# Two GNN layers on one Trainium2 core: re-ordered queues at the start, in layer 0's loop and in the last stages

## The chip, the cores and the metric

The kernel runs on one core of one Trainium2 chip. The metric is the device time of one execution in microseconds; the time before is the median of three runs. Five engines work side by side, each with an instruction queue that the program fills in order: PE multiplies matrices, DVE and POOL work on vectors, ACT applies functions, and SP issues DMAs. ACT can issue DMAs as well.

## The reference, cut to what matters

All numbers are 32-bit floats. x holds 64 batches of 256 nodes with 512 features; the adjacency is 256 x 256; attention has 8 heads of 64.

```python
# layer 0
h = relu(layernorm(x))
x = x + einsum('nm,bmd->bnd', adj, h) @ W0 + b0
# layer 1
h = relu(layernorm(x))
q, k, v = h @ Wq + bq, h @ Wk + bk, h @ Wv + bv          # 8 heads of 64
scores = q k^T / 8 + (1 - adj) * -1e9
x = x + (softmax(scores) @ v) @ Wo + bo
```

## The kernel before, in words

**Groups.** The 64 batches are worked on in 32 groups of two. Layer 0 is done for all groups first and leaves its residual and its hidden values in DRAM; layer 1 then reads them group by group.

**Products with fewer multiplications.** Almost every large product is done in a seven-product scheme of the Strassen-Winograd kind. Its operands are sums of quarters: of the weights s1 to s4, of the features t1 = b12 - b11, t2 = b22 - t1, t3 = b22 - b12 and t4 = b21 - t2. From group 2 on, layer 1 applies the scheme a second time inside some of the seven products, which are named A to G; for the output projection ("o") C, D, E and F are split again, A, B and G are not. The sums for that second level are the block sums: those of the weights are made once (`block_sums`, line 327 or 597 in the profile), those of the features per group (`Blocks.sums`, line 597).

**Clock and delays.** The program is written out by hand in steps. `tick()` ends a step; `after(n, fn)` puts an operation into the queues n ticks later, in the order of due time and then of entry. So a delay is no waiting time: it decides which instructions stand ahead of the operation in its engine's queue. `behind_seeds` and `behind_scores` are lists of work put into the queues at fixed places of `score`.

**Start.** `load(0)` issues eight DMAs of 128 KB on SP, four for each of the two batches; ACT issues the adjacency in four and then the bias. `turn_adjacency` copies and transposes the adjacency (lines 377 to 384). `first_ready` normalizes the first group tile by tile: `moments` on DVE (lines 42, 43), `power` on DVE and POOL (62, 63), `shift` on DVE (69, called nb), the ReLU on ACT (842). `first_adjacency` (line 897) then multiplies with the adjacency.

**Layer 0's loop.** In the step loop of group g, PE alternates between w_g, the weight product of group g (line 505, banks w_ga, w_gb, w_gc), and py of group g+1, its adjacency product (line 950). Meanwhile `ready(g+2, ...)` prepares the group after next: moments on DVE, the scales on POOL (lines 51 to 54), four ReLUs on ACT (871), then `feature_sums` and `last_feature_sum` on POOL (934, 937; called hs). POOL also makes t1 to t4 of y (line 498; t3 overwrites a quarter of yT and shows as yT<-yT) and, as each batch is finished, the scales of h1 (51 to 54 again, two columns wide). ACT applies h1's ReLUs (1000), DVE transposes h1 (1006, `turn`), and SP stores residual (1010) and hidden (1015) and loads a later group's x (346).

**Layer 1's loop.** For every group: two attentions (`attend`: the denominators pden at 1218, the product with v at 1225), each followed by scores (`score`, 1166) and by a stage of projections. The order within such a stage is a string of tokens: `QK`, `VO`, `V1`, and for the last stages `O1` (outputs of group 30) and `OL` (outputs of group 31). A token such as oFc is one instruction of product F of "o"; "|" is a tick; "x" is the next exponent if one is due. `score` reads its banks on DVE (1174, 1177), subtracts the upper bound "top" (1182 on DVE, 1184 or 1186 on POOL), takes exponents on ACT (1202) and sums over keys on POOL (1209). After an attention, 1/den is made (`invert`, 1240 to 1244; for the very last one partly by DVE's reciprocal, 1248), then `divide` (1263) writes OT, from which the t's of the outputs are made (`HO[g].sums`, line 498) and the block sums (`block_outputs`).

In the last group, scores come first, then four of O1's eight sections, then the last attention, then the rest of O1, and OL.

## Time and profile before

| what | us |
|---|---|
| median of 3 runs (2617.2 to 2618.22) | 2618.0 |
| the profiled execution, its own time | 2618.1 |
| its span, first to last instruction | 2616.3 |
| PE busy | 2587.3 |
| POOL busy | 2077.2 |
| DVE busy | 1910.3 |
| ACT busy | 1379.8 |

In a line of the timeline or of the groups one reads: start and duration (or busy time and mean), engine, line of the kernel, operation, written tile <- read tiles, shape, count, and in brackets how long the engine was idle before it and what ended that. A line of the waits reads: who waited, for whom, total, times, longest. A matrix product of 32-bit floats shows as two instructions. PE's ends are modelled, so its busy time can hold short waits.

### The profile page before, as it was taken

How to read it: one execution, taken by the hardware profiler on the slowest of the kernel's cores; microseconds unless marked ns; L12 is line 12 of the kernel's file. 1: busy time of each engine (PE TensorE's matmuls, PEld its weight loads, DVE VectorE, ACT ScalarE, POOL GpSimd, SP SyncE). 2: the span in 40 equal slices, each digit the busy share in tenths (PEclk: the TensorE clock that was granted, in tenths of full speed). 3: DMA queues.
4: the chain of work that ended last, by engine and by line, in shares of the span. 5: the costliest groups of instructions: out<-in, count | busy, mean ns of one | idle time of the engine just before them, and what ended most of it. 6: DMA issues, size and time to landing. Idle time of an engine off the chain costs nothing.

```text
span 2616.3 us, 57383 instructions
## 1 busy us (share of the span) xinstructions
PE 2587.3 (99%) x21876; PEld 2304.1 (88%) x21876; DVE 1910.3 (73%) x4165; ACT 1379.8 (53%) x3198; POOL 2077.2 (79%) x2259
## 2 busy tenths in 40 slices
PE   8999999999999999999999999999999999999998
PEld 7999899998888888888888888888888888888886
DVE  6888788875576677777776777777777777777776
ACT  4545454543455555555555555555555555555553
POOL 6788887774788888888877888888888888887785
PEclk9999999999999999999999999999999999999999
DMA  5776666664111222211111111111122221111101
GB/s 149 198 193 182 171 165 184 161 163 112 33 50 49 64 63 66 54 50 50 50 49 50 49 50 50 50 50 49 49 62 64 65 56 50 50 49 50 50 34 50
DMA packets 281111, 211.40 MB, mean 81 GB/s; under 512 B 145920, under 2 KB 212992, under 8 KB 280832
## 3 DMA queue, kind: packets, MB, share of 16 engines
q1 hardware_dynamic: 280224, 207.02, 29.9%
q8 instruction: 175, 2.87, 0.4%
q14 instruction: 104, 0.85, 0.1%
q10 hardware_dynamic: 608, 0.66, 0.1%
HBM read 106.96 MB, written 100.66 MB: 79 GB/s over the span
## 4 chain that ended last, share of the span: by engine, by line
PE 88%; POOL 5%; DVE 4%; DMA 2%; issue 1%; SPq 1%; ACT 1%; DVEq 0%; ACTq 0%; POOLq 0%
PE sc L1166 9%; PE pav L1225 8%; PE o_pa L662 4%; PE pden L1218 2%; PE v_pa L648 2%; PE q_pa L648 2%; PE k_pa L648 2%; PE v_pa L662 2%; PE o_pc L662 2%; PE q_pa L662 2%; PE k_pa L662 2%; PE o_pa L648 2%; PE v_pc L648 1%; PE q_pc L648 1%; PE k_pc L648 1%; DVE st L42 1%
## 5 line engine op out<-in xcount | busy, mean ns | idle before, releaser
L1174 DVE SCALAR_TENSOR_TENSOR a<-sc,top 128x512 f32<-128x512 f32 x256 | 159.0, 684 | 262.1 <-PE sc L1166 262.1
L1209 POOL TENSOR_TENSOR as<-a 128x512 f32<-128x512 f32 x256 | 320.4, 1281 | 7.8 <-ACT a L1202 6.2
L1186 POOL TENSOR_TENSOR a<-a,top 128x1024 f32<-128x1024 f32 x124 | 291.1, 2370 | 36.7 <-DVE a L1177 36.7
L1242 POOL TENSOR_TENSOR as<-as 128x512 f32<-128x512 f32 x64 | 80.9, 1264 | 275.1 <-ACT as L1241 264.3
L1202 ACT ACTIVATE a<-a 128x1024 f32<-128x1024 f32 x256 | 271.9, 1063 | 23.5 <-POOL a L1186 11.9
L1166 PE MATMUL sc<-q,k 64*128 64x256 f32 x2048 | 239.5, 383 | 0.0
L1166 PEld LDWEIGHTS sc<-q,k 64*128 64x128 f32 x2048 | 196.7, 187 | 43.3 <-issue 25.4
L1225 PE MATMUL pav<-a,v 128*32 128x256 f32 x4096 | 233.6, 379 | 0.0
L1225 PEld LDWEIGHTS pav<-a,v 128*32 128x32 f32 x4096 | 133.6, 110 | 87.8
L1232 ACT ACTIVATE as<-pden 128x512 f32<-128x512 f32 x64 | 38.3, 598 | 283.3 <-PE pden L1218 283.3
L42 DVE BATCH_NORM_STATS2 st<-x 128x6 f32<-128x512 f32 x256 | 173.2, 677 | 10.8 <-DMA x<-in_x_dram 8.0
L1177 DVE SCALAR_TENSOR_TENSOR a<-sc,maskT 128x512 f32<-128x512 f32 x256 | 158.3, 681 | 0.0
L306 ACT ACTIVATE sc<-maskT 128x512 f32<-128x512 f32 x256 | 137.5, 590 | 0.0
L1000 ACT ACTIVATE h<-x,nb,rs 128x512 f32<-128x512 f32 x128 | 97.2, 808 | 65.7 <-POOL nb L54 63.9
L871 ACT ACTIVATE h<-x,nb,rs 128x512 f32<-128x512 f32 x124 | 90.8, 803 | 65.4 <-POOL nb L54 62.3
L934 POOL TENSOR_TENSOR hs<-h 128x512 f32<-128x512 f32 x31 | 39.4, 1270 | 72.9 <-ACT h L871 71.1
L821 DVE TENSOR_TENSOR x<-o_pa,x 128x512 f32<-128x512 f32 (+1 forms) x121 | 82.4, 682 | 9.0 <-PE o_pa L662 5.2
L1263 DVE TENSOR_TENSOR oT<-pav,as 128x512 f32<-128x512 f32 x128 | 82.1, 683 | 9.2 <-POOL as L1244 9.2
L1087 ACT ACTIVATE q<-q_pa,bq_c 128x256 f32<-128x256 f32 (+1 forms) x150 | 61.7, 456 | 50.1 <-PE q_pa L648 37.6
L597 POOL TENSOR_TENSOR spare<-h1T,spare 128x128 f32<-128x128 f32 x180 | 82.2, 456 | 7.0
L1244 POOL TENSOR_TENSOR as<-as 128x512 f32<-128x512 f32 x64 | 81.0, 1265 | 5.4
L498 POOL TENSOR_TENSOR t_y<-yT,t_y 128x512 f32<-128x512 f32 (+1 forms) x65 | 82.2, 1265 | 3.4 <-ACT yT L906 1.0
(1637 smaller groups left out, 8741.1 us busy)
## 6 DMA issues: line engine op xcount, KB each, us to landing
x<-in_x_dram SPq DMA_DIRECT2D x256, 128.0 KB, 3.0
residual<-x SPq DMA_DIRECT2D x256, 128.0 KB, 2.5
hidden<-r SPq DMA_DIRECT2D x128, 256.0 KB, 4.5
h1T<-hidden SPq DMA_DIRECT2D x64, 512.0 KB, 7.4
x<-residual SPq DMA_DIRECT2D x32, 1024.0 KB, 7.9
out_dram<-x SPq DMA_DIRECT2D x62, 512.0 KB, 4.1
w_sb<-in_L_gnn_weight_dram SPq DMA_DIRECT2D x1, 1024.0 KB, 8.3
wq_sb<-in_L_gnn_Wq_dram SPq DMA_DIRECT2D x1, 1024.0 KB, 7.3
```

What stands on the lines that cost most here:

```text
L42: nc.vector.bn_stats(st, src)
L306: nc.scalar.mul(t, seed, times)
L648: nc.tensor.matmul(o[:, 0, :], lhs, rhs, start=bool(fresh), stop=True, skip_group_check=True)
L662: nc.tensor.matmul(t[:, m, :], lhs, rhs, start=starts, stop=True, skip_group_check=True)
L1000: nc.scalar.activation(h1[:, k * NT + t, :], xt[:, k * NT + t, :], AF.Relu, bias=nb[:, t:t + 1], scale=rs[:, t:t + 1])
L1166: nc.tensor.matmul(ps[j][:, kt * N:(kt + 1) * N], k[j * HD:(j + 1) * HD, c, kt * P:(kt + 1) * P], q[j * HD:(j + 1) * HD, c, :], start=(kt ...
L1174: nc.vector.scalar_tensor_tensor(o, ps[j].rearrange("p (k n) -> p k n", k=NT), SCALE, top_b[:, 0:NT, :], op0=ALU.mult, op1=ALU.subtract)
L1177: nc.vector.scalar_tensor_tensor(o.rearrange("p k n -> p (k n)"), ps[j], SCALE, maskT_f, op0=ALU.mult, op1=ALU.add)
L1186: nc.gpsimd.tensor_tensor(a, a, top_b, op=ALU.subtract)
L1202: nc.scalar.activation(a, a, AF.Exp)
L1209: nc.gpsimd.tensor_tensor(AS[c, b], a4[:, :, 0, :], a4[:, :, 1, :], op=ALU.add)
L1225: nc.tensor.matmul(po[f][h * 32:(h + 1) * 32, b * N:(b + 1) * N], v[:, k, h * HD + f * 32:h * HD + f * 32 + 32], A[h // 2, b][:, (h % 2) * ...
```

## The change

- Start: the first tile of x and the adjacency are issued alternately on SP and ACT, in the order first tile, adjacency, second tile. PE multiplies the identity by itself 11 times before the adjacency's transposes and 8 times after.
- For group 1, `shift` is put into the queue with the first ReLU instead of with the scales. Group 2's moments, scales and last feature sum take later steps.
- Layer 0: t3 is put in a tick earlier (2 instead of 3). h1's ReLUs of the batch finished second are put in a tick later, with the transposes and the store that follow them.
- `block_sums`: those of v for B, F and G go from DVE to POOL; all those of v and o are put in from tick 9 on (before from 3 and 2).
- The last two groups: group 30's block sums of the plain operand go behind 1/den; group 31's are made last operand first. For the last scores the subtraction of "top" is put in at once on POOL and at the next tick on DVE. The last t's are made in the order t2, t3, t4. DVE's reciprocal takes three quarters of the last denominators instead of two. All of O1 is put in before the last attention. O1 and OL have new orders.

```diff
@@ -233,13 +233,13 @@
     "vBj x vDc vBk vDd | vEc vDe vEd vDf vCg vp11 vCi vCh vCj vEf vCk vEe vm11 vDg | vDi vDj vEf2 vDk vDh vEi vCl "
     "vEj vEg vm10 vEk | vEl0 vEl1 vEh vEl2 ")
 O1 = (
-    "oCi oAz oCj oCk oA0 oBz oA1 x oFa | oA2 oA3 oFb x oCa oEa oFc | oFd oB0 oEb oFe op00 oB1 x oFf oCl0 oEc oFi "
-    "| oFj oCb oFg oCl1 oFk oEd oFh oCc x oCd oFl oB2 oB3 | op10 oDa op11 oG0 oDb oG1 oCe oCf | oG2 oEe oG3 oEf "
-    "oDc om11 oDd oEg oCg | oDe oDi oDf oDj oEi oEh oDk oCh oEj oEk om10 oDg | oEl oDh ")
+    "oEa oAz oA0 oBz oA1 x oB0 | oFa oCa oEb oFb oA2 x oA3 oDa oFc | oFd oB1 oFe x oB2 oFf oEc oEd oFg op00 | oB3 "
+    "oFh oFi oCb oFj op11 oFk oCc x oCd oFl | oCi oDi op10 oCj oDj oDk oDb oCk oEe oG0 oEf oCl0 oDc | oEg oG1 "
+    "oCl1 oEh oDd oG2 oCe oCf oG3 oDe | oDf oCg om11 oDg oCh oEi oDh oEj oEk om10 | oEl ")
 OL = (
-    "oAz oCi oCj oCk oA0 oBz oA1 oA2 | oA3 oFa op00 oCa oFb oB0 oCb | oEa oCl0 oFc oFd oCc oEb oFe oCd oCl1 oFi "
-    "oCe oFf oCf oFj | oFg oFk oEc oEd oFh oCg oFl oDa oB1 op10 | oB2 oB3 oDb oCh oG0 oEe op11 oDc oDd | oG1 oEf "
-    "oDe oG2 oDf oG3 oDi | om11 oEg oDj oDk oEh oDg oEi om10 oEj oEk oDh | oEl ")
+    "oAz oBz oA0 oA1 oCa oA2 | oA3 oFa oB0 oFb oB1 | oB2 op00 oDa oFc oCb oFd oB3 oFe oFi op11 oFf | oFj oFg oFk "
+    "oCi oCj oFh oDi oFl oDj oDk oEa op10 | oDb oEb oG0 om10 oDc oDd oCk oDe oEc | oDf oEd oG1 oCl0 oG2 oEe oG3 "
+    "oEf oCl1 oDg om11 oEg | oCc oCd oDh oEi oCe oEj oCf oEk oEh oCg oEl | oCh ")
 
 
 @with_exitstack
@@ -355,10 +355,15 @@
     HT = [dram.tile([P, DC, NI, GB, N // NI], F32, name=f"hidden_{g}") for g in range(NG)]
 
 
-    load(0)
+    X[0] = xpool.tile([P, T, D], F32, tag="x0", name="x_0")
     adj_r = tmp.tile([P, NT, N], F32, tag="u", name="adj_r")
+    queues = (nc.sync, nc.scalar)
     for i in range(NI):
-        nc.scalar.dma_start(adj_r[32 * i:32 * i + 32], by_block(adj, i))
+        queues[i % 2].dma_start(blocks_of(X[0], i, 0), by_block(x[0], i))
+    for i in range(NI):
+        queues[i % 2].dma_start(adj_r[32 * i:32 * i + 32], by_block(adj, i))
+    for i in range(NI):
+        nc.sync.dma_start(blocks_of(X[0], i, 1), by_block(x[1], i))
     b0_r = load_row(nc.scalar, const, b0, "b0_r")
     w0_sb = load_weight(nc, const, w0, "w0_sb")
     ident = const.tile([P, P], F32, name="ident")
@@ -571,7 +576,7 @@
                 return w[:, j, i * P:(i + 1) * P]
             s1, s2, s4 = (spare.pop(0) for _ in range(3))
             W2[n, x] = dict(a11=part(0, 0), a12=part(0, 1), a22=part(1, 1), s1=s1, s2=s2, s3=part(1, 0), s4=s4)
-            eng = nc.vector if x in "BFG" and n != "o" else nc.gpsimd
+            eng = nc.vector if x in "BFG" and n in "qk" else nc.gpsimd
             for o, p, q, op in ((s1, part(1, 0), part(1, 1), ALU.add), (s2, s1, part(0, 0), ALU.subtract),
                                 (part(1, 0), part(0, 0), part(1, 0), ALU.subtract), (s4, part(0, 1), s2, ALU.subtract)):
                 todo.append((eng.tensor_tensor, o, p, q, op))
@@ -859,8 +864,7 @@
         def scales(i):
             part, name = mv[:, i * n:(i + 1) * n, :], f"0_{g}_{i}"
             if g == 1:
-                rs = power(nc, small, mhalf, part, name)
-                h.append((rs, shift(nc, small, part, rs, name)))
+                h.append((power(nc, small, mhalf, part, name), None))
             else:
                 h.append(norm_scales(nc, small, mhalf, part, name))
             if i == 0:
@@ -868,6 +872,9 @@
 
         def relu(t):
             rs, nb = h[t // n]
+            if nb is None:
+                nb = shift(nc, small, mv[:, t // n * n:(t // n + 1) * n, :], rs, f"0_{g}_{t // n}")
+                h[t // n] = rs, nb
             nc.scalar.activation(H0[g][:, t, :], xt[:, t, :], AF.Relu,
                                  bias=nb[:, t % n:t % n + 1], scale=rs[:, t % n:t % n + 1])
 
@@ -983,8 +990,8 @@
         product(pa, "s4", "b22", False)
         nc.scalar.copy(place(0, 1), pa)
         give(pa)
-        after(1, YH[g].sums, nc.gpsimd, ("t1", "t2"))
-        after(3, YH[g].sums, nc.gpsimd, ("t3", "t4"))
+        for at, n in enumerate(("t1", "t2", "t3", "t4")):
+            after((1, 1, 2, 3)[at], YH[g].sums, nc.gpsimd, (n,))
         yield
 
     def layer0(g, seeds):
@@ -1021,7 +1028,7 @@
                 for t in range(k * NT, (k + 1) * NT):
                     moments(nc, small, mv, t, xt[:, t, :], f"1_{g}")
                 rs, nb = norm_scales(nc, small, mhalf, mv[:, s, :], f"1_{g}_{k}")
-                wait = 3
+                wait = 3 if len(done) < 4 else 4
                 after(wait, relu, k, rs, nb)
                 after(1 if len(done) < 4 else 2, leave_residual, k)
                 after(wait + 1, turn, k)
@@ -1071,8 +1078,11 @@
         both = Blocks(x, t[:, 0:2])
         last = Blocks(HO[g].all[:, 1:3].rearrange("p t c (n j) -> p t c n j", j=P), t[:, 2:4])
         if g == NG - 1:
-            both.sums(nc.gpsimd)
-            last.sums(nc.gpsimd)
+            for part in (last.one(0), last.one(1), both):
+                part.sums(nc.gpsimd)
+        elif g == NG - 2:
+            after(step, last.sums, nc.gpsimd)
+            behind_seeds.append(lambda: both.sums(nc.gpsimd))
         else:
             after(step, last.sums, nc.gpsimd)
             after(step, both.sums, nc.gpsimd)
@@ -1145,10 +1155,10 @@
     def score_bank(g, qd, c, b, **how):
         return [bank([P, NT * N], f"sc_{g}_{qd}_{c}{b}_{j}", **how) for j in range(2)]
 
-    def score_seeds(g, qd):
-        return {cb: score_bank(g, qd, *cb, seed=maskT_f, times=1.0 / SCALE) for cb in ((0, 0), (0, 1))}
-
-    def score(g, qd, sums=(5, 6, 7, 8), exps=(3, 4, 5, 8), masked=None, top_at=0):
+    def score_seeds(g, qd, n=2):
+        return {cb: score_bank(g, qd, *cb, seed=maskT_f, times=1.0 / SCALE) for cb in ((0, 0), (0, 1), (1, 0))[:n]}
+
+    def score(g, qd, sums=(5, 6, 7, 8), exps=(3, 4, 5, 8), masked=None):
 
 
         pair = [act.tile([P, GB, 2 * NT, N], F32, tag="h", name=f"a_{g}_{qd}_{c}", bufs=2) for c in range(2)]
@@ -1179,9 +1189,7 @@
                     give(ps[j])
                 if not seen:
                     if (g == NG - 1 or (g, qd) == (0, 0)) and b == 1:
-                        after(2, lambda a: nc.vector.tensor_tensor(a, a, top_b, op=ALU.subtract), a)
-                    elif top_at:
-                        after(top_at, lambda a: nc.gpsimd.tensor_tensor(a, a, top_b, op=ALU.subtract), a)
+                        after(0 if qd else 2, lambda a: nc.vector.tensor_tensor(a, a, top_b, op=ALU.subtract), a)
                     else:
                         nc.gpsimd.tensor_tensor(a, a, top_b, op=ALU.subtract)
                 if exps is None:
@@ -1244,9 +1252,9 @@
             nc.gpsimd.tensor_tensor(r, r, d, op=ALU.mult)
 
         if final:
-            for c in range(2):
+            for c in range(3):
                 nc.vector.reciprocal(rden[:, c * P:(c + 1) * P], den[:, c * P:(c + 1) * P])
-            invert(slice(N, GN))
+            invert(slice(3 * P, GN))
         else:
             behind_seeds.insert(0, invert)
         if qd == 0:
@@ -1266,10 +1274,12 @@
                 after(2, note)
             late = 6 if (g, qd) == (NG - 2, 1) else 4 if (g, qd) == (NG - 1, 0) else 0
             which = ("t3", "t2", "t4") if qd else ("t1",)
-            if late:
+            if final:
+                HO[g].sums(nc.vector, ("t2", "t3", "t4"))
+            elif late:
                 after(late, HO[g].sums, nc.gpsimd, which)
             else:
-                HO[g].sums(nc.vector if final else nc.gpsimd, which)
+                HO[g].sums(nc.gpsimd, which)
             if qd and g >= FIRST2:
                 block_outputs(g, late + 1)
 
@@ -1292,7 +1302,17 @@
     for i in range(7):
         side[20 + i].append((lambda: next(mask_steps, None),))
 
+    idle = bank([P, NT, N], "idle")
+
+    def keep_busy(n):
+
+        for _ in range(n):
+            nc.tensor.matmul(idle[:, 0, 0:P], ident, ident, start=True, stop=True)
+
+    keep_busy(11)
     turn_adjacency()
+    keep_busy(8)
+    give(idle, False)
     first_ready()
     load(1)
     ready(1, (4, 4, 4, 4), (8,), (9, 9, 9, 9))
@@ -1315,9 +1335,9 @@
             fn(*args)
 
         if g + 2 < NG:
-            ready(g + 2, (1, 1, 1, 1), (1,), (3, 3, 3, 3) if g else (4, 4, 4, 4))
+            ready(g + 2, (1, 1, 1, 1) if g else (1, 1, 2, 2), (1 if g else 3,), (3, 3, 3, 3) if g else (4, 4, 4, 4))
             after(4 if g else 5, feature_sums, g + 2)
-            after(5 if g else 6, last_feature_sum, g + 2)
+            after(5 if g else 7, last_feature_sum, g + 2)
         weighted, turned = layer0(g, seeds), adjacency(g + 1)
         for i, n in enumerate((0, 0, 1, 2, 2, 2, 0) if g == 0 else (1, 1, 2, 2, 1, 0, 0)):
             next(weighted)
@@ -1355,7 +1375,7 @@
         if g + 2 < NG:
             load_hidden(g + 2)
         if g == NG - 1:
-            score(g, 1, (2, 3, 5, 4), (1, 2, 4, 3), top_at=3)
+            score(g, 1, (2, 3, 5, 4), (1, 2, 4, 3), score_seeds(g, 1, 2))
         else:
             score(g, 1, exps=None if g + 1 >= FIRST2 else (3, 4, 5, 8))
         tick()
@@ -1371,9 +1391,9 @@
                     first = 3 * used[1]
                     KEPT[used[0]] = t[:, 0:first].rearrange("p (t q) j -> p t q j", q=3)
                 spare.extend(t[:, i, :] for i in range(first, n))
-        for n, at in (("q", 7), ("k", 16)) if g == 0 else (("v", 3),) if g == 1 else (("o", 2),) if g == 2 else ():
+        for n, at in (("q", 7), ("k", 16)) if g == 0 else (("v", 9),) if g == 1 else (("o", 9),) if g == 2 else ():
             for i, work in enumerate(block_sums(n)):
-                after(at + i // (2 if n == "v" else 4), *work)
+                after(at + i // (8 if n == "v" else 4), *work)
         if g + 1 < FIRST2:
             for which in queries_keys(g + 1):
                 run(plain(g + 1, *which))
@@ -1385,10 +1405,11 @@
             run(follow(steps, QK))
         else:
             last = follow(quartered_outputs(g - 1), O1)
-            run(last, 4)
+            run(last)
         attend(g, 1)
         if g + 1 < NG:
-            score(g + 1, 0, (5, 6, 7, 8) if g + 1 < NG - 1 else (1, 1, 1, 1), None if g + 1 >= FIRST2 else (3, 4, 5, 8))
+            score(g + 1, 0, (5, 6, 7, 8) if g + 1 < NG - 1 else (1, 1, 1, 1), None if g + 1 >= FIRST2 else (3, 4, 5, 8),
+                  score_seeds(g + 1, 0, 2) if g + 1 == NG - 1 else None)
             tick()
 
             def multiplied(g=g):
@@ -1419,7 +1440,7 @@
                     run(steps)
             if g < FIRST2:
                 run(plain_outputs(g, seeds))
-    run(last)
+    tick()
     last = follow(quartered_outputs(NG - 1), OL)
     run(last, 2)
 
```

## The prediction

> **What bounds the kernel now.** The page first: PE is busy 2587.3 of 2616.3 us, so no edit that leaves the matmuls alone can win more than the 29.0 us in which PE is idle, plus matmuls that run slowly while counted as busy. The second view is the table of stretches, to find where those 29 us lie (columns: length; busy time and count of PE, PEld, DVE, ACT, POOL; granted clock, DMA share, GB/s):
>
> ```profile
> PE 2587.3 (99%) x21876; PEld 2304.1 (88%) x21876; DVE 1910.3 (73%) x4165; ACT 1379.8 (53%) x3198; POOL 2077.2 (79%) x2259
> 0.00:60.00 60.00, 47.89 (x259) 41.97 (x260) 37.42 (x81) 27.46 (x42) 36.44 (x52) 1.00 0.57 143
> 700.00:760.00 60.00, 58.02 (x480) 49.30 (x480) 43.14 (x85) 29.87 (x74) 50.61 (x63) 1.00 0.20 54
> 2580.00:2600.00 20.00, 16.42 (x140) 13.01 (x140) 12.35 (x24) 4.74 (x11) 13.28 (x15) 0.86 0.06 24
> 2600.00:2616.40 16.40, 10.42 (x72) 9.22 (x70) 9.75 (x27) 0.90 (x3) 0.00 (x0) 0.89 0.30 105
> ```
>
> Idle: 12.1 us in the first 60, 2.0 in 700:760, 2.9 in 2560:2580, 3.6 in 2580:2600, 6.0 after. From 880 to 2540 there is none. Third, PE's own waits:
>
> ```profile
> PE o_Fs L648 <- ACT o_F L685: 2.9, 1, 2.9
> PE py L897 <- ACT h L842: 2.8, 1, 2.8
> PE o_Es L648 <- DVE x L821: 2.8, 1, 2.8
> PE w_0a L505 <- DVE x L821: 1.7, 1, 1.7
> PE q_pb L648 <- DVE q_F L821: 1.4, 1, 1.4
> PE pden L1218 <- POOL as L1209: 1.4, 2, 0.8
> ```
>
> Fourth, the timeline of layer 0, because one wait there hides in the busy time:
>
> ```profile
> 140.60 0.22 POOL L51 TENSOR_SCALAR rs<-mv 128x2 f32<-128x2 f32 x1
> ...
> 142.14 1.28 POOL L498 TENSOR_TENSOR yT<-yT 128x512 f32<-128x512 f32 x1
> 143.38 1.27 POOL L498 TENSOR_TENSOR t_y<-yT,t_y 128x512 f32<-128x512 f32 x1
> 143.47 1.99 PE L505 MATMUL w_6c<-w_sb,yT 128*128 128x256 f32 x8
> 144.74 0.23 POOL L51 TENSOR_SCALAR rs<-mv 128x4 f32<-128x4 f32 x1
> 146.71 2.93 ACT L871 ACTIVATE h<-x,nb,rs 128x512 f32<-128x512 f32 x4 [2.29 <-POOL nb L54]
> 149.72 1.27 POOL L934 TENSOR_TENSOR hs<-h 128x512 f32<-128x512 f32 x1 [1.82 <-ACT h L871]
> ```
>
> w_6c starts 0.05 us after t3 (the "yT<-yT" on POOL) ends. The next group's t3 ends at 162.11, 18.69 later; nearly every t3 from 50.00 to 592.43 stands about 18.69 after the one before. Groups without a wait take 18.34 (w_17a 342.54 to w_18a 360.88). So **POOL, in a loop with ACT, sets the pace of layer 0**: scales of group g+2 at 144.74, their four ReLUs, the feature sums at 149.72, t1 and t2, two sets of h1 scales, t3, t4: 18.69. PE's bias product at 284 puts it 3 us behind, and it catches up 0.35 a group until 470.
>
> **What the Trainium skill says.** (1) "TensorE: Matmul & The Clock Gate", Part 1: an idle window of about 3.4 us halves the clock. Agreed: the granted clock is 0.86 in 2580:2600, and pairs of 128x128 products after the stall at 2578.7 start 0.43 us apart, 0.22 elsewhere. (2) "SBUF — State Buffer", SBUF: two separate sides: a VectorE operation with two SBUF inputs and a GpSimd one exclude each other for a whole instruction. Agreed: the 128x4 nb (L69) beside POOL's t3 took 1.21 us, the 128x1 ones 0.15 to 0.40; two 128x128 sums on DVE (L327) at 732.7 took 1.72 and 2.33. (3) "Trainium Kernel Development and Optimization", Key Constraints: several issuing queues save issue time only. Agreed: from 2 to 20 us the DMA share is 0.79 or more.
>
> **The change, part by part.**
>
> *Start.* x's first tile now goes by SP and ACT, then adjacency, then the second tile. Landings before: x 3.49, 4.37, 5.46, 7.39 (its fourth piece was issued only at 3.51, as the first landed). In bytes, the first tile is complete after 512 KB, which was 5.46; adjacency after 768, about 6.4 against 5.88; the second tile after 1280 to 1536, 8.5 to 9.6 against 9.61. Eleven products of 128x128 (0.43 us each at the slow clock, estimated from 2580) run 1.4 to about 6, eight more after the transposes. The first product starts near 9.2 instead of 10.48, and its stage, whose 32 instructions took 9.51 us with the slow clock up to 15.2, ends near 16 instead of 20. **Most of this is hidden**: the next group's x is bound by bytes and still lands at 18.8. What is left: POOL's power for that group runs at 20.8 instead of 22.1, since t_y no longer stands before it; nb, now behind the x add on DVE, comes near 22.2 and may be locked out until t3 ends, 23.2; the ReLUs start 23.25 against 24.41. Gain 1.2 us; 0 if x lands later by that, 2.1 without the lock. The 1.7 us wait of w_0a goes too (its add stood behind nb), but PE then waits for hs(1), so this is inside the 1.2 and not beside it. The idle products have a cost if the clock is still slow after the transposes: eight then last 3.4 us instead of 1.8 and the first product starts at 11.4, 0.9 later than now; its stage would still end by 18.5, under the same cover, group 1's x. So they are worth 0, and their bounds are 0 and 0.
>
> *Group 0.* Two moments of group 2 and its scales come one and two steps later; on POOL they still follow hs(1) directly: nothing. hs4(2), 1.27 us, falls behind t1 and t2, which ends the 0.7 us wait of w_1a; it then stands ahead of t3, needed later.
>
> *t3 a step sooner.* It passes the second h1 scales: 140.60 to 142.14, 1.54 us. The loop has the same sum, so this is not 0.35 a group but one advance, until the next wait: t2, ready at 138.81 and used at 139.73, 0.9 us of slack. PE runs 0.9 us earlier against POOL. In the last group, without adjacency between, the wait for t3 (608.36, 0.3 plus the 0.3 of slow restart) goes: 0.6. Sum 1.5.
>
> *h1's second ReLUs a step later* (with its transposes, and leave_hidden on SP one step on). On ACT they now follow the copy L969 and stand before L871: they would run 143.5 to 145.0, L871 starts 146.7. Cover 1.6 us. In group 14, where PE is late (L969 ended 296.16, L871 began 296.55), it is short by 0.3: -0.3 once. load(g+3) waits up to 1.5 us longer for these ReLUs, and what stands behind it on SP with it; its x is first read over 10 us later: nothing.
> Layer 0: 1.2 + 1.5 - 0.3 = **2.4** (0.5 to 4).
>
> *Sums of v and o.* Twelve 128x128 sums of v leave DVE, where the locked ones held q_F: PE's 1.4 plus 0.3 with slow restarts, 2.3 from 737 to 739. POOL gets 24 x 0.46 = 11 us at steps 9 to 11, about 746 to 757, after the key sums and before 1/den (760.17, POOL waited 8 us there): covered; without that cover, the denominators of the next attention would be late by up to 3. The sums of o (16 x 0.46) leave the way of the key sums for which pden waited 0.6 at 818.9; used in the following stage, 10 us later. **2.6** (1 to 3.3).
>
> *The last stages.* PE needs per 128x256 step 0.43, per 128x128 step 0.223; O1 and OL have 12 and 28 each, 11.4 us; an attention 4.45. From 2570.9, where O1 begins, that is 11.4 + 4.45 + 11.4 = 27.3, to 2598.2; it took to 2610.4. The 12.2 us are the two waits of 2.9 and 2.8, the pden wait, the slow clock twice, and gaps inside.
> Before, eight block sums of 0.73 stood on POOL ahead of 1/den of (31,0) (2565.6 to 2571.5); four now stand behind it: 1/den ends 2571.9 against 2574.9, the divide moves from 2574.9 to about 2574.6 (DVE's scores and the subtraction, now first, are next in line), O1's adds start 2575.8 against 2577.3. POOL's subtraction of (1,0) runs at 2575 instead of 2579.7, so the key sums end near 2582.4.
> All of O1 now runs before the last attention: 2570.9 + 11.4 + about 1 for seeds and adds = 2583.3, above the key sums; attention to 2587.8. DVE has no adds left over: it finishes three reciprocals (0.88 each) by 2587.8, the divide by 2589.1 (before 2591.7, behind O1's adds), t2, t3, t4 at 0.7 each by 2591.1. Meanwhile PE has A0, A1, then Ca after the first divide, A2, A3, Fa after t2, B after t3: 3.9 us of work in 4.4 us. OL's adds, 8 to 9 us on DVE after 2591.1, and PE's 11.4 with about 1.6 of waits (the last t4 of the C and E sums comes at 2596.6), both end about 2601 to 2602. DVE ended at 2611.5: 9.4 less after a final add and DMA that now follow the split store. I take 2 off for semaphore steps that I can't place: **7.4** (4 to 9.4).
>
> Sum: 2.4 + 2.6 + 7.4 = 12.4. The profiled execution took 2618.1, 1.8 over its span; the median is 2618.0, so I carry it over unchanged: **2605.6**.
>
> **Rivals.**
> *Bare last stage.* With O1 gone ahead, nothing covers the divide: if Fa and B wait for t2 and t3 in a row, PE idles as long as before (2.8) and the clock falls again (some 1.7 us lost, as in 2595.7 to 2599). The tail then gives 3: 2610. For it: OL's B and D stand early. Against: A and the 2 us earlier divide.
> *Front hidden.* Only layer 0's 2.4 is lost, because x lands later with the new order or POOL stays in step: 2608. For it: the bytes are the same.
> *A longer loop (slower).* ACT is strictly in order. If h1's second ReLUs, behind L969, held L871, each of some 28 groups would grow by the hold, as L871 is in the loop. It decides from 12.4 / 28 = 0.44 us a group, that is when the pair ends 1.6 + 0.44 = 2.0 us later than I put it. At a hold of 1 us: +28 - 12.4, 2634. For it: the thin 0.35 us in group 14; against: 1.6 in the bound groups.
> *Nothing moves.* The stalls return in other places: 2618.
>
> **How the numbers follow.** About 5 us, 0.2%, is what a measurement can tell. Likeliest case 0.62, bare tail 0.17, front hidden 0.10, longer loop 0.06, nothing 0.05. The first three are faster: 0.89 in all, less 0.01 where their shortfalls join; nothing and that remainder, 0.06, are within 0.2%; the loop is slower, 0.06. The range runs from 2601.5 (3.8 in layer 0, 3.3, 9.4) to 2611.5 (0.5, 1, 5, or the bare tail with less in front).
>
> **What would show it.** Right: t2, not t3, ends just before its product in groups 6 to 13; the period stays 18.69; no DVE sum near 732; O1 finished before the last attention, its divide by 2589 less the shift, clock 1.00 after 2560. Wrong: a period over 18.7, PE waiting for hs or h in mid-layer, or an idle window after the last attention.

## The result, and the profile after

The changed kernel took 2605.2 us (median of five runs, 2604.6 to 2606.0) beside 2618.0 for the kernel before: a ratio of 0.9952, 95% interval 0.9938 to 0.9967. The profiled execution took 2605.4, its span 2603.7. The forecast of 2605.6 hit the total, but two of its three terms did not: layer 0 gave 2.5 (forecast 2.4), the sums of v and o 4.6 (2.6), the last stages 5.4 (7.4). Two errors of 2 us cancel, and inside layer 0 a start that was put too high and a t3 that was put too low cancel as well (below). That the total is right to 0.4 us is luck.

These terms come from laying the two traces side by side: how much sooner does the same product start after than before? The first weight product of group 2 is 0.65 us ahead, of groups 6 to 13 about 1.2, of group 30 1.58, the first attention 2.53, the fourth 5.81, the seventh 7.14, the last but one 7.27, the end of the span 12.66.

First the page's sum and the same kind of stretches as before:

```profile
PE 2586.1 (99%) x21914; PEld 2303.6 (88%) x21914; DVE 1908.9 (73%) x4154; ACT 1381.1 (53%) x3198; POOL 2082.9 (80%) x2275
0.00:60.00 60.00, 52.65 (x300) 46.25 (x301) 38.06 (x83) 27.39 (x42) 37.59 (x52) 1.00 0.57 140
700.00:760.00 60.00, 60.00 (x512) 51.65 (x511) 39.07 (x80) 30.71 (x75) 57.51 (x78) 1.00 0.20 54
2560.00:2580.00 20.00, 19.02 (x164) 15.62 (x164) 17.24 (x34) 7.97 (x16) 16.54 (x15) 1.00 0.06 22
2580.00:2600.00 20.00, 15.87 (x122) 12.33 (x114) 15.74 (x35) 2.84 (x9) 7.96 (x15) 1.00 0.25 88
```

PE has no idle time left in 700:760, and the granted clock is 1.00 up to the end of its work. The 4.8 us more of busy time in the first row are no gain: the 19 products of the identity alone show as busy for 6.1 us. Read a stretch for what it still waits for, not for its busy share. Four lines of PE's waits:

```profile
PE w_0a L510 <- DVE x L826: 1.4, 1, 1.4
PE py_1a L957 <- ACT h L878: 1.2, 2, 0.9
PE o_pa L667 <- DVE x L826: 0.7, 1, 0.7
PE o_Fs L653 <- ACT o_F L690: 0.4, 1, 0.4
```

The 2.9 us for ACT's o_F is 0.4 now; o_Es, q_pb and pden are gone. In the loop of layer 0 the timeline shows the change of guard:

```profile
137.47 1.27 POOL L503 TENSOR_TENSOR t_y<-yT,t_y 128x512 f32<-128x512 f32 x1
138.79 1.99 PE L510 MATMUL w_6a<-w_s,t_y 128*128 128x256 f32 x8
140.38 1.27 POOL L503 TENSOR_TENSOR yT<-yT 128x512 f32<-128x512 f32 x1
142.40 1.89 PE L510 MATMUL w_6c<-w_sb,yT 128*128 128x256 f32 x8
```

t2 (the first line) ends at 138.74 and its product starts 0.05 later, while t3 now has 0.75 us to spare. The next group's t2 stands 18.68 after: the period has not moved.

### The profile page after: what moved, and what is told of

Its sections match the earlier page's. It is cut to its first block, busy times and chain, and to the rows that moved or that the text cites. A ratio compares the mean times of both kernels' runs of the same rounds, so it can differ in the third digit from the quotient of the medians.

```text
span 2603.7 us, 57470 instructions
## 1 busy us (share of the span) xinstructions
PE 2586.1 (99%) x21914; PEld 2303.6 (88%) x21914; DVE 1908.9 (73%) x4154; ACT 1381.1 (53%) x3198; POOL 2082.9 (80%) x2275
## 4 chain that ended last, share of the span: by engine, by line
## 5 line engine op out<-in xcount | busy, mean ns | idle before, releaser
L1250 POOL TENSOR_TENSOR as<-as 128x512 f32<-128x512 f32 x64 | 80.5, 1258 | 267.3 <-ACT as L1249 263.8
L1013 DVE STREAM_TRANSPOSE r<-h 128x512 f32<-128x512 f32 x128 | 84.5, 691 | 8.9 <-ACT h L1007 3.6
```

Source lines behind the costliest of these rows:

```text
L1013: nc.vector.transpose(r[:, :, k, t, :], h1[:, k * NT + t, :].rearrange("p (j b) -> p j b", b=32))
```

## The experiments

Each run is compared with runs of the kernel before on the same chip. That one took 2617.4 to 2617.6 there, except beside e9, e10 and e11, where its 30 runs lie between 2617.4 and 2622.2 with a median of 2620.2; for those the ratio counts. The changed kernel's ratio is 0.9952, and its 2605.2 stood beside 2618.0, so a difference of times and one of ratios can be 0.5 to 1 us apart. The interval of a ratio of five to seven runs reaches 3 to 4 us to either side: differences of 2 to 5 us below rest on the traces laid side by side, not on the ratios alone.

In the recorded expectations TensorE is PE, GpSimd POOL, VectorE DVE, ScalarE ACT and SyncE SP. The edits are given in short form, partly in words: "-" is the changed kernel, "+" the run.

### The four parts undone, one at a time

**e1**, the start as before:
```
-keep_busy(11); turn_adjacency(); keep_busy(8)
+turn_adjacency()
-x's first tile and adj alternating on SP and ACT, then the second tile
+load(0) on SP; adj on ACT
```


> The changed kernel with the start of before: x and adjacency issued as before, no idle products. Theory (the parts add up, and the start is covered: in the changed kernel the feature sums of group 1 begin on POOL at 27.37, against 27.42 before): no change from the changed kernel, 2605.2 us within 0.5, and w_2a starts where it does in the changed kernel, 59.7 within 0.3. Rival (the warm clock and the earlier x carry through): slower by 1.2 or more, 2606.4 or above.

Measured 2605.3 (ratio 0.9954, 0.9941 to 0.9968): the start is worth 0.1 us by the times, 0.5 by the ratios, less than these runs can tell. The first weight product comes 2.16 us later than in the changed kernel (19.97 against 17.81) and that of group 1 0.29 us earlier (40.72 against 41.01). So in this pair of profiles 2 us are won in group 0 and lost again before group 1. DVE's timeline of the changed kernel, and below it two lines of the kernel before, show where:

```profile
16.00 0.87 DVE L478 TENSOR_TENSOR w_s<-w_sb 128x512 f32<-128x512 f32 x1 [2.45 <-DMA w_sb<-in_L_gnn_weight_dram]
16.91 1.10 DVE L478 TENSOR_TENSOR w_s<-w_s,w_sb 128x512 f32<-128x512 f32 x1
17.93 0.68 DVE L42 BATCH_NORM_STATS2 st<-x 128x6 f32<-128x512 f32 x1
```
```profile
14.35 0.69 DVE L473 TENSOR_TENSOR w_s<-w_sb 128x512 f32<-128x512 f32 x1 [1.05 <-DMA w_sb<-in_L_gnn_weight_dram]
16.67 0.69 DVE L42 BATCH_NORM_STATS2 st<-x 128x6 f32<-128x512 f32 x1 [0.90 <-DMA x<-in_x_dram]
```

w0 landed at 15.98; before, at 14.33. DVE waits 2.45 us for it, its sums stand ahead of group 1's moments, and these start at 17.93 where they started at 16.67. Group 1's ReLUs come at 24.36; before, at 24.41.

One pair of profiles would not show this, since w0's landing varies by itself (12.15 in e1, with the start of before). But in the eleven profiles with the new start w0 landed between 13.76 and 16.03, and group 1's ReLUs came 8.2 to 9.0 us after it each time, at 22.76 to 24.92 with a median of 23.81. Group 1's x follows w0 on the same queue, so w0's bytes and its two sums on DVE are not told apart. With the old start (before and e1) the ReLUs came at 24.41 and 24.08, because POOL reached power only at 22.11 and 21.77.

**e2**, t3 and h1's second ReLUs at their old steps:
```
-after((1, 1, 2, 3)[at], ...)      wait = 3 if len(done) < 4 else 4
+after((1, 1, 3, 3)[at], ...)      wait = 3
```


> The changed kernel with t3 put in at step 3 and the second ReLUs of h1 at step 3, as before. Theory (POOL's loop of 18.69 us sets the pace, t3 a step sooner is one advance up to t2's slack): slower by about 1.0, 2606.2 us: w_a of groups 6 to 22 starts some 0.6 later than in the changed kernel, and the last group's wait for t3 returns (0.4); every loop keeps its 18.69. Rival (the wait of 0.33 is saved in each of the groups that had it): slower by 16 x 0.33 = 5.3, 2610.5.

Measured 2607.8 (0.9963, 0.9950 to 0.9977), 2.6 us more than the changed kernel; the theory's 1.0 was too small and the rival's 5.3 too large. The run takes back both edits and does not separate them. t3 is the late one again (it ends at 142.82, its product starts at 142.88), with a period of 18.69. This run's start happened to be 0.55 sooner; net of that, the edit is worth 1.1 to 1.2 us in groups 6 to 13, 1.6 in group 30 and 2.5 at the first attention, where the short waits of the last group and of k_0a return. It is one advance and some of the hand-over to layer 1, not a gain for each group.

**e3**, the block sums of v and o as before:
```
-eng = nc.vector if x in "BFG" and n in "qk" else nc.gpsimd;  v and o from step 9
+eng = nc.vector if x in "BFG" and n != "o" else nc.gpsimd;  v from step 3, o from step 2
```


> The changed kernel with the block sums of v and o as before (v's B, F and G on DVE, from step 3; o's from step 2). Theory (read from the two traces: attentions 0 to 6 gain 4.6 between them, all by these sums): slower by 4.6, 2609.8 us, with the wait of q_pb for q_F back. Rival (the sum of the prediction, 2.6; the rest came of other things that moved, the seeds or the shift of layer 0): 2607.8.

Measured 2609.4 (0.9969, 0.9958 to 0.9980): 4.2 us, the theory's size. The waits that come back:

```profile
PE q_pb L653 <- DVE q_F L826: 1.4, 1, 1.4
PE pden L1226 <- POOL as L1217: 0.6, 1, 0.6
```

They sum to 2.0, but between the third and the fourth attention 3.3 us are lost and between the sixth and the seventh 1.37: more than the list of waits names. Product by product against the changed kernel, 2.3 of the 3.3 us are lost from q_pb to q_Cs (733.9 to 736.0), the rest mostly at k_Ds, q_pa and k_Es (749.0 to 751.3), where the gaps that show are 0.11 us or less.

**e4**, the last stages as before (the orders O1 and OL, the place of the last attention, the order of the block sums and of the last t's, the subtractions of "top", the reciprocals):

> The changed kernel with the last stages of before (orders O1 and OL, half of O1 after the last attention, the block sums ahead of 1/den, the subtractions of top, the reciprocals and the order of the last t's). Theory (from the traces: the attentions before the last keep a lead of 7.27, the end has 12.66): slower by 5.4, 2610.6 us, with both waits of 2.8 and the slow clock back. Rival (the sum of the prediction): slower by 7.4, 2612.6.

Measured 2609.6 (0.9970, 0.9959 to 0.9982): 4.4 us. Both waits of the kernel before are back:

```profile
PE o_Fs L653 <- ACT o_F L690: 2.8, 1, 2.8
PE o_Es L653 <- DVE x L826: 2.8, 1, 2.8
```

From the last attention but one to the end it takes 51.48 us; the kernel before took 53.54, the changed one 48.15. Of the 2 us between the first two, the slow clock accounts for most (estimated at 1.7 us a window, see the end): two windows of it in the tail before, one in this profile. The profiled execution was the fastest of e4's seven, 1.6 us under their median.

Undone singly, the four cost 0.1 + 2.6 + 4.2 + 4.4 = 11.3 of 12.8 us by the times and 0.5 + 2.9 + 4.5 + 4.7 = 12.6 by the ratios, where the whole change is 12.6: no remainder is shown. The new steps of group 0 were in no run of their own. In every profile that has them, w_2a follows w_1a after 18.65 to 18.69 us (before, 19.26); in e2, with the start's chance taken off, this lead of 0.6 is down to 0.06 at group 6, because PE meets POOL there anyway.

### What sets the pace of layer 0

**e5** and **e6** each change one number of the changed kernel, **e8** both:
```
e5: after((1, 1, 2, 3)[at]     ->  after((1, 1, 2, 4)[at]          (t4)
e6: after(5 if g else 7, last_feature_sum  ->  after(7, last_feature_sum   (hs4)
```


> The changed kernel with one number altered: layer 0's t4 is made at step 4 of the group instead of step 3, so that on GpSimd the scales of group g+2 stand ahead of it. Theory (GpSimd's own round of a group sets the loop of groups 6 to 13, 18.68 us against some 18.35 us of TensorE's work): the scales no longer wait behind t4, GpSimd's idle time inside the round goes, the loop falls towards TensorE's 18.35 us, and some 14 loops x 0.33 = up to 4.5 us are gained on the changed kernel, about 2600.7 us. Rival (the loop is TensorE's own, or t2 and t3 are what is late and t4 never was): 2605.2 within 0.5, with the loop still 18.68 us. A third answer, t4 now late for its own product: slower, by up to 0.7 us per group.

> The changed kernel with the last feature sum of group g+2 (hs4) made at step 7 in every group, where the changed kernel has it at step 7 in group 0 alone and at step 5 in the others. Theory (t2 is late by where it stands in GpSimd's queue, and the sum ahead of it costs 1.27 us once): t1, t2 and t3 are ready up to 1.2 us sooner in groups 6 to 13, the loop keeps its 18.68 us, and the gain is once up to 1.2 us: 2604.0 to 2605.2 us. Rival (each group gains anew, because the loop itself gets shorter): up to 14 x 0.33 = 4.6 us, 2600.6. Other side: hs4 becomes late for its own product in the next group, and TensorE waits for it: 2606 or more.

> Both of these one-number edits together: t4 at step 4 and hs4 at step 7. If GpSimd's round sets the loop, the two gains add where they lie in different places: up to 4.5 + 1.2 us, 2599.5. If only the place of t2 in the queue counts: 2604. If t4 or hs4 become late for their own products: 2606 or more.

e5: 2603.4 (0.9949, 0.9935 to 0.9962). It fits neither answer. POOL's queue shows why: step 4 put t4 behind the scales in group 1 alone. That gave a lead of 1.2 us once (t2 of group 2 ends 2.2 us sooner, 1.0 of it by the start); t2 then ended at 61.78, 80.47, 99.17, 117.84 and 136.52, every 18.7 us as ever. PE ran through groups 2 to 7 in 18.34 each, had used up the lead by about group 8 and fell into step again.

e6: 2599.8 (0.9935, 0.9921 to 0.9948), 5.4 us better than the changed kernel by the times, 4.5 by the ratios: the rival's size, not the single lead of 1.2. Its profile started 1.6 us sooner at group 2, which is chance (below); from there to the first attention it gains 4.5. t2 ends at 153.91, 172.48, 191.04 and 209.61, 18.57 apart. PE at 18.34 a group catches up with it only at group 12. The traces suggest where the 0.11 us come from: in the changed kernel hs4 stands right behind the sum that it reads, and the two start 1.35 us apart (77.49 and 78.84); in e6 t1 stands there, which does not read that sum, and follows after 1.23 (57.21 and 58.44).

So there are two loops, each with a beat of its own, and the table of waits does not show the slower one. In groups 2 to 4 of the changed kernel PE waits for nothing, and yet t2 ends every 18.67 to 18.69 us. Here are t2 on POOL and the first weight product on PE, for groups 3 and 4:

```profile
81.42 1.28 POOL L503 TENSOR_TENSOR t_y<-yT,t_y 128x512 f32<-128x512 f32 x1
100.10 1.28 POOL L503 TENSOR_TENSOR t_y<-yT,t_y 128x512 f32<-128x512 f32 x1
```
```profile
78.03 1.89 PE L510 MATMUL w_3a<-w_sb,yT 128*128 128x256 f32 x8
96.37 1.89 PE L510 MATMUL w_4a<-w_sb,yT 128*128 128x256 f32 x8
```

POOL's two stand 18.68 us apart, PE's two 18.34. POOL's timeline in group 3:

```profile
90.35 0.20 POOL L54 TENSOR_TENSOR nb<-nb,rs 128x4 f32<-128x4 f32 x1
93.59 1.27 POOL L941 TENSOR_TENSOR hs<-h 128x512 f32<-128x512 f32 x1 [3.04 <-ACT h L878]
```

The last scale ends, four ReLUs on ACT follow, and POOL waits 3.04 us for them. With 15.6 us of POOL's own work, its short gaps included, that is 18.68. POOL and ACT wait for each other in a ring that runs free of PE, and PE meets it when its lead is gone. In groups 4 to 19 a weight sum of 1.28 us (line 478) stands in that pause at no cost: 1.81 us of waiting are left and the period is the same. That names the lever: to shorten the ring, work has to move *into* the pause, behind the scales.

**e12** does that: t4 at step 5, behind the scales of g+2 in every group.

> The changed kernel with t4 at step 5, which puts it on GpSimd behind the scales of group g+2 in every group (step 4 did so in group 1 alone). In the changed kernel t2 ends every 18.67 to 18.69 us from group 2 on, also in groups 2 to 5 where TensorE needs 18.34 and does not wait: a ring of its own on GpSimd and ScalarE, 15.6 us of GpSimd's work and 3.04 us in which it waits for the four ReLUs that follow the last scales. Theory (the ring sets the loop once TensorE has used up its lead): t4 now runs inside the 3.04 us, the ring falls to about 17.4 us, t2 is ready early in every group, all loops are 18.34 us, and about 4.5 us are gained on the changed kernel: a ratio to the kernel before of about 0.9935 where the changed kernel has 0.9952, 2600.7 us where before takes 2617.6. Rival (what moves in the queue gives a lead once, and the round stays 18.68): 1.3 to 1.8 us, a ratio of 0.9946. Other side: t4 is 2.1 us later, of some 4 us that it had before its product; if that is short, TensorE waits for it and the kernel is slower than the changed one.

Measured 2600.7 (0.9936, 0.9922 to 0.9950), the ring theory's figure. The interval still reaches the rival's 0.9946; it is the trace that decides. POOL in group 10:

```profile
215.96 0.20 POOL L54 TENSOR_TENSOR nb<-nb,rs 128x4 f32<-128x4 f32 x1
216.11 1.29 POOL L478 TENSOR_TENSOR wk_sb<-wk_sb 128x512 f32<-128x512 f32 x1
217.35 1.28 POOL L503 TENSOR_TENSOR t_y<-yT,t_y 128x512 f32<-128x512 f32 x1
219.62 1.27 POOL L941 TENSOR_TENSOR hs<-h 128x512 f32<-128x512 f32 x1 [0.99 <-ACT h L878]
```

Between the scales and hs there are now 3.46 us, 2.6 of them filled with work. In groups 6 to 13 t2 is ready 2.8 to 3.2 us ahead of its product and stays so, where the rival's single lead would shrink by 0.34 a group; the groups take 18.34 us (group 9 took 18.66), and the first attention starts 4.7 us sooner than in the changed kernel. Starting from the same start as that (40.96 and 41.01 in group 1), this profile is the cleanest of the three.

e8: 2600.5 (0.9935, 0.9922 to 0.9949), no better than e6 alone: once PE sets the pace, more lead buys nothing. (Its profile lost 2 us at the start.)

### The last stages taken apart

**e7** keeps the new orders and moves the last attention back to where it was; **e9** keeps the new place with the old orders and releases; **e10** keeps both and takes back the releases alone.
```
e7:  -run(last); attend(g, 1); ... tick()
     +run(last, 4); attend(g, 1); ... run(last)
e9:  O1, OL, block sums, last t's, subtraction, reciprocals of before; run(last) ahead of attend
e10: block sums, last t's, subtraction, reciprocals of before; O1, OL and the place as changed
```


> The changed kernel, its new orders of the last output products kept, but only four of the steps of O1 ahead of the last attention and the rest behind it, as the kernel before has it. It asks what of the 5.4 us of the last stages is the place of the attention and what is the order of the products. Theory (order and the divided sums' release count, the place does not): 2605.2 within 1 us, since the products that are moved cover the wait behind the attention. Rival (the place counts: the last attention is what everything in the end waits for, and moving it sooner or later carries the end with it): with the attention some 6 us sooner the divide is done some 6 us sooner, but the last products start later; slower by 2 to 4 us, 2607 to 2609.

> Of the change in the last stages the place alone: all of O1 ahead of the last attention, as the changed kernel has it, with the orders O1 and OL, the block sums' order, the seeds and the last sums and reciprocals of the kernel before. The other three corners are known: both new 2605.2, both old 2609.6, new orders with the old place 2613.4. Theory (the place is the part that gains, because it takes the work out of the stretch in which the tail waits, and the orders and releases only shorten the wait ahead of it): 2606 to 2608. Rival (place and orders only fit each other: either alone is worse than neither): 2610 or more, since the old O1 was written for products that lie behind the attention and will wait for the old sums in front of it. Neither counts alone and they add: about 2601, which the three corners leave out.

> The changed kernel with its new orders and the new place kept, but what releases their operands as before: GpSimd makes the four block sums in the old order and at the old step, the last scores are seeded as before and their subtraction is at step 3 on GpSimd, the last attention inverts N columns at once, and its three sums are DVE's plain call. Theory (the new orders ask for certain operands early and these edits are what makes them early): TensorE waits for DVE's x and for GpSimd's sums in O1 and the time is 2607 to 2610. Rival (the releases are small change, the orders do it): 2605.2 within 1 us.

"Releases" are the edits that decide when an operand is ready: block sums, last t's, subtraction, reciprocals. The seeds that two expectations name are no difference: `score` makes the same two by itself.

| kernel | orders | place | releases | ratio (95%) | last attention but one to the end, us | PE's gaps in it, us | slow windows in it |
|---|---|---|---|---|---|---|---|
| before (profile) | old | old | old | 1 | 53.5 | 6.5 | 2 |
| e4 | old | old | old | 0.9970 (0.9959 to 0.9982) | 51.5 | 6.4 | 1 |
| changed | new | new | new | 0.9952 (0.9938 to 0.9967) | 48.2 | 2.2 | 0 |
| e7 | new | old | new | 0.9984 (0.9978 to 0.9991) | 56.5 | 7.7 | 2 |
| e10 | new | new | old | 0.9980 (0.9973 to 0.9987) | 53.2 | 7.9 | 0 |
| e9 | old | new | old | 0.9996 (0.9988 to 1.0005) | 59.2 | 10.4 | 4 |

(Before has all the old steps, e4 only those of the tail, so the ratios of these two differ by the other parts.) My theory for e7, that the place does not count, was wrong by 8 us; for e9 the rival was right; e10 came out slower than either of its answers (0.9980 of 2617.5 is 2612). In each of these three mixtures the tail of the profile is longer than in e4. By the ratios e9 is clear of e4 and e7 nearly so, while e10's interval overlaps with e4's; e10's profile, like e9's, was the fastest of its runs, 4.1 us under their median. The slow clock (see the end) hides how alike the mixtures are: with 1.7 us taken off for each slow window, an estimate, the two old tails are near 50 us, the changed one 48 and all three mixtures 52 to 53. The waits name the missing half. In e7 the attention comes too soon for its key sums:

```profile
PE pden L1226 <- POOL as L1217: 3.4, 2, 3.0
PE o_Cs L653 <- DVE x L826: 2.7, 1, 2.7
```

In e9 PE stands still for 2.85 and 1.92 us in O1, now all of it ahead of the attention, so that the attention starts 28.6 us after the one before it (22.1 in the changed kernel); behind it nothing is left to cover the divide (1.84) and POOL's block sums (3.7). In e10 PE waits 2.6 us in O1 for ACT's o_F, and the new OL asks for a sum that the old releases give late, at 2592.70. The first of these lines of the waits is e9's, the second e10's:

```profile
PE o_pb L653 <- POOL spare L602: 3.7, 1, 3.7
```
```profile
PE o_Fs L653 <- POOL spare L602: 3.2, 1, 3.2
```

The three other mixtures (new releases with the old orders, in either place, and the new orders alone) were not tried.

### An attempt on the start

**e11**: e6, with w0 on ACT's queue ahead of b0.
```
-b0_r = load_row(nc.scalar, ...);  w0_sb = load_weight(nc, ...)        # w0 on SP, behind x
+nc.scalar.dma_start(w0_sb, ...);  b0_r = load_row(nc.scalar, ...)
```


> The changed kernel with hs4 at step 7 (2599.8 us) and, in the start, w0 loaded by ScalarE's queue ahead of b0 instead of by SyncE's behind x. In the changed kernel's profile w0 landed at 15.98 us, 1.65 us later than before, and DVE's two sums of its blocks stand ahead of group 1's moments; that is where the sooner first product was lost. Theory (w0 is what holds group 1): w0 lands some 4 to 6 us sooner, group 1's moments start when its x has landed, and 1 to 2 us are gained: 2598 to 2599. Rival (group 1's x or the chain of scales on GpSimd holds it, or the start is covered whatever is done there): 2599.8 within 0.6.

Measured a ratio of 0.9947 (0.9933 to 0.9960), against e6's 0.9935: no gain, and more likely a loss of 2 to 3 us, though the intervals overlap. (Three runs took 2604.1 to 2604.2, two 2607.1 and 2608.4; the profile is of the one with 2607.1.) w0 landed 3.6 us sooner than in the changed kernel (12.43; 13.76 in e6's profile), but it is 1024 KB and went ahead of x's second tile, of which three quarters landed at 12.74 to 14.62 (in the changed kernel the whole at 6.21 to 9.79). PE's wait for it:

```profile
PE py L905 <- ACT h L848: 5.4, 1, 5.4
```

The first weight product started at 24.80 instead of 18.26, and the clock was slow once more from 14.5 to 21.3. So the run does not say what a sooner w0 is worth with x left where it was.

## Why the prediction was right or wrong

- **What bounds the kernel.** Right: POOL with ACT sets layer 0's pace, and PE falls back on it. What the prediction did not draw from its own finding is that work put into POOL's pause is free; e12 shows 4.5 us lying there. The signs that it named came true (t2 ends just before its product, the period is 18.68, the clock is 1.00 to the end of PE's work), but for the last divide: it ended at 2583.58, 1.8 us after 2589 less the shift.
- **Start, 1.2: too large.** It is worth 0.1 to 0.5 in e1 and 0.07 at group 1 in this pair of traces; at the median of the eleven profiles with it, group 1's ReLUs are 0.3 to 0.6 ahead of the two with the old start. The step that failed is "the ReLUs start 23.25": it moved POOL's power to 20.8 because t_y no longer stood before it, and overlooked that w0 is behind x in SP's queue and that its two sums stand ahead of the moments on DVE. The last moment ended at 21.3 (20.6 before), the power ran from 21.7 to 23.1, and nb took 1.22 us beside t3, the lock that was forecast. The zero for the idle products is not contradicted, but e1 undid them with the queues and does not separate the two.
- **t3 a step sooner, 1.5: right in kind.** The advance ends at t2, and by e2 it is 1.1 to 1.2 us in groups 6 to 13, where the forecast had 0.9. Group 0's 0.6 at group 2 comes on top of nothing: it uses up part of the same slack of t2. The drift to group 30 (0.3 to 0.4) and the hand-over to layer 1 (0.95, forecast 0.6) bring e2's 2.6. The -0.3 for group 14 does not show: the lead there is 1.28, as in groups 6 to 13. The longer loop did not come either; the period stayed at 18.68.
- **Sums of v and o, 2.6: too small by 2.0.** The term counted the 2.3 near 738 and part of the 0.6 before pden. It came to 3.3 and 1.35 us in the two places. The 2.3 near 738 were right; another 1.0 was lost at 752 to 755, at k_Ds, q_pa and k_Es, whose gaps show as 0.11 or less, and the pden wait of 0.6 cost 1.35 with the products around it. PE's idle time in 700:760 was only 2.0, and part of the loss lay inside its busy time. A term for a stall that takes only the idle time of the table was a lower bound here. The cover for the 24 sums on POOL was there: they run from 743.97 to 754.68, straight before 1/den.
- **The last stages, 7.4: too large by 2.0.** O1, put at 11.4 and about 1, took 13.94, so the last attention starts at 2577.57 where the forecast, shifted by the lead of 7.27, has 2576.0. The reciprocals, the divide and the t's follow. Three lines of the changed kernel, and one of the kernel before:

```profile
2566.14 1.75 DVE L1192 TENSOR_TENSOR a<-a,top 128x1024 f32<-128x1024 f32 x1
2582.29 1.29 DVE L1271 TENSOR_TENSOR oT<-pav,as 128x512 f32<-128x512 f32 x2
2584.82 0.94 DVE L503 TENSOR_TENSOR t_o<-oT,t_o 128x512 f32<-128x512 f32 x1
```
```profile
2576.14 1.22 DVE L1182 TENSOR_TENSOR a<-a,top 128x1024 f32<-128x1024 f32 x1
```

 The first is the subtraction of "top", which took 1.22 before and stands here beside POOL's sums: the exclusion that the Trainium skill describes in "SBUF — State Buffer" (SBUF: two separate sides), priced for layer 0 but not for this place. (Before, DVE's subtraction began 0.25 us ahead of POOL's key sums, and it was these that took longer, 3.32 us for two where the next two took 2.50.) The t's are done at 2585.76, 1.9 after the shifted forecast. OL then lost about 1.1, and from DVE's last add to the end of the span 5.8 us pass instead of 4.83. Together 4.0 us, where 2 had been taken off.
- **The rivals.** Bare last stage: no; PE idles 2.2 us in the tail and the clock holds. Front hidden: half true, since the start was hidden and the rest of layer 0 was not.

## What to carry to other kernels

Where two loops of slightly different length run side by side (here 18.34 and 18.68 us), look at the period of the one that is *not* waited for yet; the waits show it only once the lead is gone. Shorten the slower ring by moving work into its own pause: one number did that here for 4.5 us, and the fastest versions measured, e6 and e12, differ from the changed kernel by one number each (0.9935 and 0.9936, not to be told apart). Orders of products, the place of a stage and the releases of its operands are best taken as one edit: here the three mixtures that were tried had a longer tail than the old one in their profiles (e10 not clear of it by its ratio), and undoing one piece says what the fit is worth, not what the piece is worth.

## What the runs showed of the hardware

- The slow clock came in windows of 3.413 us or multiples of it: before, at 2578.65 and 2595.72, which are five windows apart. Such a window costs about 1.7 us, an estimate from half its length.
- How long PE stood still inside one window decided about the next. I laid this grid over all 14 profiles. Of the windows at full clock, all 10607 with up to 1.72 us of PE idle were followed by another one at full clock (26 of them had over 1.0), and all 19 with more, from 1.72 us up, by a slow one. That is about half a window, and less than the idle window of about 3.4 us with which the prediction reckoned. So the same stall can cost nothing or 1.7 us. e4 had two of nearly the same length:

```profile
2570.64 0.49 PE L653 MATMUL o_Fs<-spare 128*128 128x128 f32 x2 [2.85 <-ACT o_F L690]
2586.37 0.49 PE L653 MATMUL o_Es<-spare,spare 128*128 128x128 f32 x2 [2.81 <-DVE x L826]
```

 The first lay in one window, and the clock was slow from 2571.15 on. The second fell on a border (2584.80) and left 1.24 and 1.57 us in its two windows: the clock stayed. In e10's profile stalls of 2.62 and 3.18 us, both on borders, cost no clock. The tail before paid for two windows, e4's for one, e7's for two, e9's for four. e7's 21 runs spread over 5 us and e10's 18 over 7, which this would explain; that is not shown, since one run of each has a trace.
- The first eleven products of the identity had the clock at full speed from 4.4 us on in the changed kernel, and from 4.2 to 7.2 in the eleven other profiles that have them; without them it came at 15.2 (before) and 14.9 (e1). It bought little, since the first stage was not what group 1 waited for.
- The start differs from run to run: group 2's first weight product started between 58.1 and 60.2 us in eleven profiles with the same start, and the later w0 had landed, the later it was, nearly in order. A single profile can't tell an edit of 1 us there; the medians can.
